# Two-layer graph attention on Trainium2: a divided tile's two sums are joined on TensorE instead of VectorE in the first half of layer 0

## The chip, the cores and the metric

The kernel runs on one core of one Trainium2 chip (trn2). A core has four engines that compute, each with its own queue of instructions, and SyncE (SP), which issues DMAs. The four are TensorE (PE, matrix products, which it adds up in PSUM), VectorE (DVE), ScalarE (ACT) and GpSimd (POOL), and POOL's queue also issues the gathers of this kernel. In the profile PEld is the loading of the stationary operand of a matmul. Each engine takes its queue in order, and waits on semaphores for the others. A layer's data pass from DRAM to the on-chip SBUF and PSUM; PSUM is where matmuls write.

The metric is device time in microseconds (us) of the whole program. The kernel before takes 2428.36 us, the median of three runs (2426.71 to 2430.07).

## The reference, cut to what matters

`x` is 8 batches of 2048 nodes with 256 features, in fp32. `adj` is a 2048 x 2048 matrix of 0 and 1 with few ones (about 17 in a row, the diagonal among them). Two layers of attention over the neighbours follow one another, each with a residual and a layer norm:

```python
    def _L0_gnn_ref(inp, adj, W1, W2, W3):
        h1 = jnp.einsum('bnc,cd->bnd', inp, W1)
        h2 = jnp.einsum('bnc,cd->bnd', inp, W2)
        h3 = jnp.einsum('bnc,cd->bnd', inp, W3)
        e = jnp.einsum('bnd,bmd->bnm', h1, h2)
        e = jax.nn.leaky_relu(e, ALPHA)
        e = jnp.where(adj[None, :, :] > 0, e, NEG_INF)
        attention = jax.nn.softmax(e, axis=-1)
        h_prime = jnp.einsum('bnm,bmd->bnd', attention, h3)
        return jax.nn.relu(h_prime)
    ...
    x = _layernorm(x + _L0_gnn_ref(x, adj, L0_gnn_W1, L0_gnn_W2, L0_gnn_W3), axis=-1)
    x = _layernorm(x + _L1_gnn_ref(x, adj, L1_gnn_W, L1_gnn_a), axis=-1)
```

The change is in layer 0. It has one attention head (layer 1 has four), and its weights multiply whole feature rows of the neighbours. Since the sum over neighbours and the product with `W3` can change places, the kernel adds up weighted rows of `x` and multiplies the sum with `W3` afterwards.

## The kernel before

**Tiles and units.** `fast_path` sorts the nodes by their number of neighbours and takes them in 16 tiles of 128 nodes, t = 0 (most neighbours, 36) to t = 15 (fewest, 11); `SLOTS` holds the largest number of each tile. The 8 batches are two halves of 4. A unit is one layer, one half and one tile: 16 units of layer 0's first half (h = 0) with t from 15 down to 0, 16 of its second half, then 32 of layer 1. In the first half VectorE also makes the list of neighbours of each tile out of a row of `adj` (`neighbours`, L613 to L631); the second half and layer 1 use the same lists.

**A slot** is the k-th neighbour of all 128 nodes of a tile. POOL gathers its 128 rows (4 batches x 256 features, 512 KB) into one of 19 ring buffers that hold two slots each (`gather`, L203). VectorE makes four dot products of it with the node's own vector `g` (`dots`, L721). When a part of a unit has all its slots, VectorE and ScalarE make the softmax weights of them. ScalarE then builds, for each slot and batch, a diagonal matrix of weights (`weighted`, L931). TensorE multiplies the gathered rows with the diagonals and adds them up in PSUM (`add_slot`, L895: eight matmuls of 64 x 64 by 256 columns a slot, four at a time in the four quarters of the array). When a chunk's last slot has been added, its ring buffer is free for the next gather.

**Divided units.** In layer 0 a unit with 16 slots or more is divided into two parts, t = 10 down to 0 in each half. The second part's softmax has a new maximum and sum, so the first part's result is a share of the whole. `sums0` runs over both parts; each has its own pair of accumulators (`u.accs[0]` and `u.accs[1]`, two PSUM tiles of 128 x 512). At the fifth slot of the second part, ScalarE scales the first part's accumulators by these shares into the buffer `u.hs` in SBUF (L1018). After the last slot, `whole` in `after0` has VectorE add the second part's accumulators to `u.hs` (L1032, two instructions). An undivided unit (t = 15 to 11) has its one pair copied out by ScalarE (L1036).

**After the sum.** `turn_h` transposes `u.hs` on TensorE (L1046), ScalarE copies the transposes out (`hT`), `project_h` multiplies with `W3` (the matmuls of L509 that write `ps_p_h`), and `residual` on VectorE applies the relu, adds the node's own row and takes the statistics (L1056, L1059). Then come the norm on ScalarE (L487), another transpose, the queries of layer 1 (`queries`, L1095) and their scatter to DRAM. Before a unit's slots `before0` does the like for `g`: `project` (the matmuls of L509 that write `ps_p_g`) and a ScalarE copy (L712).

**The order.** All engines' instructions are written out in an order made by hand. `tick` is called once for each slot of the current unit's sum; in each tick come the next slots' dot products (of later units), the next diagonals, and whatever is due. `due(n, f)` puts `f` into the order n ticks later. `after0` is called when a unit's last slot has been added, and for a divided unit sets

```python
        at = 4 if split else 2
        due(at, whole)
        due(at + 2, turn_h)
        due(at + 6, project_h)
```

so these come among the next unit's slots. `residual` is due 3 and 4 ticks after `project_h`. The instructions of one engine run in this order; between engines only data and buffers make them wait.

**The general path.** If the fast path finds that its tables don't hold the graph, it sets `flag`, and `general_path` computes everything densely. `Weights` prepares the weights for both: `products()` makes `W1 W2^T`, `terms()` makes the columns of `W` and `a` for layer 1's attention terms.

Of the kernel before, what the change touches and what calls it, by code (L numbers as in the profile page):

```python
# [139 lines left out]
def fast_path(  # L140
# [24 lines left out]
    nc = tc.nc  # L165
    B, N, C = x.shape
# [6 lines left out]
    HW = HC // 2  # L173
# [58 lines left out]
    w = Weights(nc, const, wp, ps_tile, w1, w2, w3, wq, a, C, "", (kept[:, 0], kept[:, 1]))  # L232
    ident = w.ident
# [11 lines left out]
    for it in range(NT):  # L245
        r = ring_tile(f"adj_{it}")
# [122 lines left out]
    for b in range(4):  # L369
# [6 lines left out]
        for it in range(4 * b, 4 * b + 4):  # L376
            nc.tensor.matmul(
                pm,
                lhsT=which[:, it, :],
                rhs=homes[:, it, :2].rearrange("p f s -> p (f s)"),  # L380
                start=(it == 0),
                stop=False,
# [3 lines left out]
                lhsT=which[:, it, :],  # L386
                rhs=homes[:, it, 2],
                start=False,
                stop=(it == NT - 1),
# [21 lines left out]
    for r in range(2):  # L411
        rr = slice(64 * r, 64 * r + 64)
        pr = ps_tile(f"ps_half_{r}")[:, :NT]
        for c in range(2):
            nc.tensor.matmul(
                pr[64 * c : 64 * c + 64],
                lhsT=ident[rr, rr],
                rhs=ranked[rr, 0, :],
                start=True,
                stop=True,  # L420
                tile_position=(64 * r, 64 * c),
# [70 lines left out]
    def due(distance, stage, *args):  # L492
        heappush(events, (clock[0] + distance, len(stamps), partial(stage, *args)))
        stamps.append(None)
# [406 lines left out]
                        tile_position=(64 * r, 64 * c),  # L901
                    )

    def add_extra(acc, rows, lhsT, width):
        for r in range(2):
            for j in range(2 * C // width):
                for c in range(2):
                    rhs = rows[:, ts(2 * c + j, C)]
                    if width > C:
                        rhs = rows[:, ts(c, 2 * CD)].rearrange("p (j w) -> p j w", j=2)[:, :, :C]  # L910
                    nc.tensor.matmul(
                        acc[r][64 * c : 64 * c + 64, ts(j, width)],
                        lhsT=lhsT(r, c, j),
                        rhs=rhs,
                        start=False,
                        stop=(j == 2 * C // width - 1),
                        tile_position=(0, 64 * c),
                    )

# [74 lines left out]
    def sums0(u):  # L994
        u.accs = []
        for i, part in enumerate(u.parts):
            acc = None
            for k in range(part.K):
                while len(u.diags) <= part.at + k:
                    yield 0  # L1000
                if acc is None:
                    acc = [acc_tile(f"acc_{u.name}_{i}_{r}") for r in range(2)]
                diag = u.diags[part.at + k]
                c, s = part.where(k) if k < part.main else (0, 0)
                rows, n, _ = u.chunks[i][c]
                if k < part.main:
                    add_slot(acc, k, part.K, rows[:, s, :], diag)
                else:
                    add_extra(
                        acc, rows[:, 0, :], lambda r, c, j: diag[r][:, 2 * c + j, :], C  # L1010
                    )
                if s == n - 1:
                    credits[0] += 1
                if i == 1 and k == 4:
                    u.hs = hs_rows
                    for r in range(2):
                        for j in range(2):
                            nc.scalar.activation(  # L1018
                                u.hs[:, ts(2 * r + j, C)], u.accs[0][r][:, ts(j, C)], AF.Copy,
                                scale=u.fs[:, r, j : j + 1],  # L1020
                            )
                yield 1
            u.accs.append(acc)

    def after0(u):
        h, t, n = u.h, u.t, u.name

        def whole():
            if len(u.parts) == 2:
                for r in range(2):  # L1030
                    v = u.hs[:, ts(r, HW)]
                    nc.vector.tensor_tensor(v, v, u.accs[1][r], ALU.add)  # L1032
            else:
                u.hs = hs_rows
                for r in range(2):
                    nc.scalar.copy(u.hs[:, ts(r, HW)], u.accs[0][r])  # L1036

        def turn_h():
            u.hT = wide_tile(f"hT_{n}")
            by_node = u.hT[:, :HC].rearrange("p (c j k r n) -> p j (k r) c n", c=2, j=2, k=KC, r=2)  # L1040
            for j in range(2):
                pt = ps_tile(f"ps_t_h_{n}_{j}")
                for k in range(KC):
                    for r in range(2):
                        o = r * HW + j * C + k * P
                        nc.tensor.transpose(pt[:, ts(2 * k + r, P)], u.hs[:, o : o + P], ident)  # L1046
                due(2, nc.scalar.copy, by_node[:, j], pt.rearrange("p (a c n) -> p a c n", a=4, c=2))

        def project_h():
            u.y = wide_tile(f"y0_{n}")[:, :HC]  # L1050
            u.yb = u.y.rearrange("p (b c) -> p b c", b=HB)
            u.st = sp.tile([P, 2, nc.vector.BN_STATS_DIM], F32, tag="st", name=f"st_{n}")
            project(u.hT, w.w3, f"h_{n}", 3, residual)

        def residual(i, pp):
            nc.vector.scalar_tensor_tensor(  # L1056
                u.y[:, ts(i, 512)], pp, 0.0, u.xr[:, ts(i, 512)], ALU.max, ALU.add
            )
            nc.vector.bn_stats(  # L1059
                u.st[:, i, :], u.yb[:, 2 * i : 2 * i + 2, :].rearrange("p b c -> p c b")  # L1060
            )
            if i == 1:
                mv = u.st.rearrange("p i (b s) -> p (i b) s", s=3)
                u.mv = mv[:, :, 1], mv[:, :, 2]
                rested[u.index] = clock[0]
                due(2, roots)

        def roots():
            u.z = root(u.mv, n)
            due(2, scales)  # L1070

        def scales():
            u.scales = factors(u.mv, u.z, n)
            due(2, norms, 0)
            due(3, norms, 2)

        def norms(b0):
            for b in (b0, b0 + 1):
                normalise(u.yb, u.yb, b, *u.scales)
            if b0:  # L1080
                nc.sync.dma_start(x1s[h][ts(t, P), :], u.y)
                due(2, turn_x)

        def turn_x():
            u.x1T = wide_tile(f"x1T_{n}")
            turn(u.y, f"x1_{n}", u.x1T)
            due(4, queries, 0)
            due(6, queries, 1)

        def queries(r):  # L1090
            u.qrow = q_rows
            for b in range(2 * r, 2 * r + 2):
                pq = ps_tile(f"ps_q_{n}_{b}")
                for k in range(KC):
                    nc.tensor.matmul(  # L1095
                        pq[:, : CD + H],
                        lhsT=u.x1T[:, ts(b * KC + k, P)],
                        rhs=w.sqs[:, k, : CD + H] if b == 0 else w.sqs[:, k, H:],
                        start=(k == 0),
                        stop=(k == KC - 1),  # L1100
                    )
                if b in (0, HB - 1):
                    o = 0 if b == 0 else H + b * CD
                    due(2, nc.scalar.copy, u.qrow[:, o : o + CD + H], pq[:, : CD + H])
                    continue
                o = 2 * H + HB * CD + (b - 1) * H
                due(2, nc.scalar.copy, u.qrow[:, H + b * CD :][:, :CD], pq[:, :CD])
                due(2, nc.scalar.copy, u.qrow[:, o : o + H], pq[:, CD : CD + H])
            if r == 1:
                due(3, own_terms)  # L1110

        def own_terms():
            own, o = own_d[h][ts(t, P), :], H + HB * CD
            nc.sync.dma_start(own[:, :H], u.qrow[:, :H])
            nc.sync.dma_start(own[:, H : HG - H], u.qrow[:, o + H :])
            nc.sync.dma_start(own[:, HG - H :], u.qrow[:, o : o + H])
            late.append((clock[0] + 1, store))

        def store():
            scatter(f"q{h}", qg[h][:, :], order[:, t : t + 1], u.qrow[:, H : H + HB * CD])  # L1120
            tabled[0] += 1
            if tabled[0] == 2 * NT:
                credits[0] += MORE

        split = len(u.parts) == 2
        at = 4 if split else 2
        due(at, whole)
        due(at + 2, turn_h)
        due(at + 6, project_h)
# [328 lines left out]
    for j, u in enumerate(units):  # L1458
# [9 lines left out]
        if 2 <= j < 10:  # L1468
            b, i = divmod(j - 2, 2)
# [22 lines left out]
def general_path(  # L1492
# [36 lines left out]

    w = Weights(nc, const, tp, ps_tile, w1, w2, w3, wq, a, C, "g")  # L1530
    w.products()
    w.rows_of(nc, const, 1, C)
    ident = w.ident
    mask = maskp.tile([P, NT, N], I8, tag="mask", name="gmask")
# [252 lines left out]
```

## Time and profile before

| What | Before |
|---|---|
| Timed runs, median (lowest to highest) | 2428.36 us (2426.71 to 2430.07) |
| Profiled execution, time | 2403.25 us |
| its span, first to last instruction | 2401.5 us |
| granted TensorE clock, mean | 0.899 |
| DMA moved | 717.85 MB, mean 299 GB/s |
| dot products L721 | 2248, 421 ns each |
| diagonals L931 | 2248, 344 ns each |
| matmuls of slots in layer 0, L895 with `dg` | 8992, 392 ns each |
| additions L1032 | 44, 681 ns each |

The profiled execution is one run, 25 us shorter than the median of the timed ones. The mean duration of a matmul is its time in a pipeline: in dense stretches several run at once. Layer 0's first half ends about 800 us into the span, its second half about 1375 us, and layer 1 takes the rest.

How to read the views used below. The totals give each engine's busy time, its share of the span and its number of instructions. A window gives the same between two points of time. A group names line, engine, operation and `out<-in` by the program's tile names, with the number of instructions, then busy time, mean duration in ns, and the idle time of that engine just before them with what ended it. `held` is the name under which the trace has `u.hs`, `u.g` and the query rows, which share three set-aside ring buffers; `s` is a gathered slot, `dg` a diagonal, `ident` the identity matrix. A wait names the waiting instruction, `<-`, and the one that released it.

### The profile page before, as it was taken

The numbers are of one execution on the slowest core, as the hardware profiler recorded it, in microseconds if no ns is written. First come the engines' busy times: TensorE is split into PE (matmuls) and PEld (weight loads), VectorE is DVE, ScalarE is ACT, GpSimd is POOL, SyncE is SP. The second block draws the span as 40 slices with busy tenths as digits, with TensorE's granted clock in tenths as the row PEclk, the third lists the DMA queues.
The fourth block names the chain that finished last, engine by engine and source line by source line (L and its number), as shares of the span: only waits on it lengthen the run. The fifth ranks groups of instructions, "written<-read, shape, count | busy, mean of one in ns | idle before, by whom it ended". The sixth has DMA issues, their size and how long they took to land. (4 is left out here: it accounts for less than half of the span.)

```text
span 2401.5 us, 50494 instructions
## 1 busy us (share of the span) xinstructions
PE 2006.4 (84%) x16234; PEld 1068.8 (45%) x16234; DVE 1950.7 (81%) x6799; ACT 1411.2 (59%) x4867; POOL 1407.8 (59%) x1379
## 2 busy tenths in 40 slices
PE   5158999899889999999999888888888788777885
PEld 2135566565555666666666532332233232222232
DVE  7498699988888886988989578787977788788887
ACT  6045676666667778777777655443465556343545
POOL 3354465645545556555555566666666666766663
PEclk9578999999999999999999989788888888978887
DMA  9977898878868889888888899889999899999981
GB/s 378 380 246 263 277 331 305 311 277 287 297 228 279 290 291 315 278 280 302 292 312 282 289 344 318 310 296 337 320 316 334 300 342 308 313 315 326 327 308 53
DMA packets 229919, 717.85 MB, mean 299 GB/s; under 512 B 47824, under 2 KB 57168, under 8 KB 227216
## 3 DMA queue, kind: packets, MB, share of 16 engines
q0 software_dynamic: 182272, 645.78, 76.6%
q1 hardware_dynamic: 46144, 67.65, 8.4%
q8 instruction: 132, 2.16, 0.4%
q10 hardware_dynamic: 1232, 1.11, 0.1%
q14 instruction: 139, 1.14, 0.1%
HBM read 674.46 MB, written 76.02 MB: 313 GB/s over the span
## 5 line engine op out<-in xcount | busy, mean ns | idle before, releaser
L895 PE MATMUL acc<-s,ident 64*64 64x512 f32 x4496 | 804.7, 687 | 179.7 <-issue 135.0
L203 POOL DMA_INDIRECT s<-xg,idx x564 | 591.9, 1049 | 518.1 <-PE acc L895 262.6
L721 DVE CUSTOM_DVE_ANT_0 j<-s,held 128x256 bf16<-128x256 f32 x2248 | 798.9, 421 | 54.6 <-DMA s<-xg,idx 42.9
L895 PE MATMUL acc<-s,dg 64*64 64x256 f32 x8992 | 682.3, 392 | 92.7 <-issue 42.3
L203 POOL DMA_INDIRECT s<-qg,idx x564 | 574.1, 1018 | 299.1 <-issue 150.8
L931 ACT ACTIVATE dg<-twice,e 128x64 f32<-128x64 f32 x2248 | 575.1, 344 | 64.7 <-remote 23.0
L895 PEld LDWEIGHTS acc<-s,ident 64*64 64x64 f32 x4496 | 284.3, 151 | 688.2 <-issue 608.5
L978 DVE TENSOR_TENSOR s<-s,p 128x2048 f32<-128x2048 f32 (+1 forms) x246 | 542.9, 2210 | 0.1
L895 PEld LDWEIGHTS acc<-s,dg 64*64 64x64 f32 x8992 | 377.8, 134 | 352.6 <-issue 159.0
L968 ACT ACTIVATE s<-s,e 128x64 f32<-128x64 f32 x1376 | 344.8, 342 | 81.1 <-DVE e L1234 23.4
L721 DVE DVE_READ_ACCUMULATOR2_ANT e<- 128x1 f32 x2248 | 184.1, 82 | 0.1
L211 POOL DMA_INDIRECT out_dram<-o,oidx x128 | 130.1, 1017 | 70.6 <-issue 31.6
L1436 ACT ACTIVATE e<-e 128x40 f32<-128x40 f32 (+19 forms) x88 | 27.7, 315 | 212.6 <-DVE m L1213 73.1
L1095 PE MATMUL ps_q<-wqs,x1T 128*128 128x264 f32 x512 | 138.8, 412 | 9.8 <-ACT held L1436 6.0
L509 PE MATMUL ps_p_g<-held,xT 128*128 128x256 f32 x512 | 125.7, 395 | 17.8 <-ACT xT L1436 16.3
L509 PE MATMUL ps_p_h<-held,hT 128*128 128x256 f32 x512 | 122.2, 392 | 0.1
L1436 ACT COPY held<-ps_q 128x4 f32<-128x4 f32 (+1 forms) x192 | 51.1, 311 | 115.4 <-PE ps_q L1095 96.5
L1095 PEld LDWEIGHTS ps_q<-wqs,x1T 128*128 128x128 f32 x512 | 95.4, 196 | 50.2 <-issue 22.7
L509 PEld LDWEIGHTS ps_p_g<-held,xT 128*128 128x128 f32 x512 | 97.3, 196 | 45.5 <-ACT xT L1436 16.8
L1158 DVE TENSOR_TENSOR e<-s,own 128x32 f32<-128x32 f32 (+1 forms) x290 | 52.9, 187 | 70.8 <-DMA s<-qg,idx 58.5
L509 PEld LDWEIGHTS ps_p_h<-held,hT 128*128 128x128 f32 x512 | 96.6, 194 | 26.2 <-issue 12.9
L1336 DVE TENSOR_TENSOR xr<-xr,ex 128x1024 f32<-128x1024 f32 x32 | 39.3, 1227 | 75.9 <-issue 53.0
(210 smaller groups left out, 1513.9 us busy)
## 6 DMA issues: line engine op xcount, KB each, us to landing
adj<-in_adj_dram SPq DMA_DIRECT2D x16, 1024.0 KB
x1s<-y SPq DMA_DIRECT2D x32, 512.0 KB
xr<-x1s SPq DMA_DIRECT2D x128, 128.0 KB
s<-xg,idx POOLq DMA_INDIRECT x564
s<-qg,idx POOLq DMA_INDIRECT x564
edges<-adj SPq DMA_DIRECT2D x16, 512.0 KB
xg<-in_x_dram SPq DMA_DIRECT2D x4, 2048.0 KB
xg<-in_x_dram POOLq DMA_DIRECT2D x8, 1024.0 KB
```

The lines of the kernel that those rows point to most:

```text
L203: nc.gpsimd.indirect_dma_start(out=dst, out_offset=None, in_=table, in_offset=AT(ap=index, axis=0), bounds_check=table.shape[0] - 1, oob_i ...
L211: ins = nc.gpsimd.indirect_dma_start(out=table, out_offset=AT(ap=index, axis=0), in_=src, in_offset=None)
L509: nc.tensor.matmul(pp[:, ts(j, C)], lhsT=srcT[:, ts((2 * i + j) * KC + k, P)], rhs=weight[:, k, :], start=(k == 0), stop=(k == KC - 1),)
L721: nc.vector.tensor_tensor_reduce(out=jt, in0=rows[:, ts(b, C)], in1=others(b), scale=1.0, scalar=0.0, op0=ALU.mult, op1=ALU.add, accum_out ...
L895: nc.tensor.matmul(out, lhsT=lhsT, rhs=rhs, start=(k == 0 and j == 0), stop=(k == K - 1 and (j == 1 or diag is None)), tile_position=(64 * ...
L931: nc.scalar.activation(diag[:, b, :], twice, AF.Copy, scale=u.p[i][:, b, k : k + 1])
L968: nc.scalar.activation(v[:, a, g, :], v[:, a, g, :], AF.Copy, scale=pv[:, a, g : g + 1])
L978: nc.vector.tensor_tensor(v, v, pv.unsqueeze(3).to_broadcast([P, n, H, D]), ALU.mult)
L1095: nc.tensor.matmul(pq[:, : CD + H], lhsT=u.x1T[:, ts(b * KC + k, P)], rhs=w.sqs[:, k, : CD + H] if b == 0 else w.sqs[:, k, H:], start=(k = ...
L1158: nc.vector.tensor_tensor(e[:, k : k + ns, :].rearrange("p s (b g) -> p s b g", b=HB), rows[:, :ns, :].rearrange("p s (b w) -> p s b w", b ...
L1336: nc.vector.tensor_tensor(u.xf, u.xf, u.ex, ALU.subtract)
L1436: heappop(events)[2]()
```

## The change

For a divided unit of the first half (`joined`), the last slot of the second part no longer closes the accumulation: `add_slot` and `add_extra` leave the stop flag off. A new step `join`, due at once after the unit's last slot, has TensorE multiply `u.hs` with the identity into the second part's accumulators: four matmuls with 128 rows, 64 stationary columns and 512 moving columns, two for each of the two accumulators, in the left and the right half of the array. `whole`, due four ticks after as before, then copies the two accumulators to `u.hs` on ScalarE in place of the two additions on VectorE. Units of the second half, undivided units and layer 1 keep their code. In the built program 44 matmuls (in 22 pairs) and 22 copies are added, 22 additions are gone, and everything else of the fast path stands in its old order. `general_path` now calls `w.terms()`, which adds instructions behind the branch to it.

```diff
@@ -901,7 +901,10 @@
                         tile_position=(64 * r, 64 * c),
                     )
 
-    def add_extra(acc, rows, lhsT, width):
+    def joined(u):
+        return u.h == 0 and len(u.parts) == 2
+
+    def add_extra(acc, rows, lhsT, width, last=True):
         for r in range(2):
             for j in range(2 * C // width):
                 for c in range(2):
@@ -913,7 +916,7 @@
                         lhsT=lhsT(r, c, j),
                         rhs=rhs,
                         start=False,
-                        stop=(j == 2 * C // width - 1),
+                        stop=(last and j == 2 * C // width - 1),
                         tile_position=(0, 64 * c),
                     )
 
@@ -1003,11 +1006,12 @@
                 diag = u.diags[part.at + k]
                 c, s = part.where(k) if k < part.main else (0, 0)
                 rows, n, _ = u.chunks[i][c]
+                last = not (i == 1 and joined(u))
                 if k < part.main:
-                    add_slot(acc, k, part.K, rows[:, s, :], diag)
+                    add_slot(acc, k, part.K + (not last), rows[:, s, :], diag)
                 else:
                     add_extra(
-                        acc, rows[:, 0, :], lambda r, c, j: diag[r][:, 2 * c + j, :], C
+                        acc, rows[:, 0, :], lambda r, c, j: diag[r][:, 2 * c + j, :], C, last
                     )
                 if s == n - 1:
                     credits[0] += 1
@@ -1025,8 +1029,23 @@
     def after0(u):
         h, t, n = u.h, u.t, u.name
 
+        def join():
+            for r in range(2):
+                for c in range(2):
+                    nc.tensor.matmul(
+                        u.accs[1][r][64 * c : 64 * c + 64, :],
+                        lhsT=ident[:, ts(c, 64)],
+                        rhs=u.hs[:, ts(r, HW)],
+                        start=False,
+                        stop=True,
+                        tile_position=(0, 64 * c),
+                    )
+
         def whole():
-            if len(u.parts) == 2:
+            if joined(u):
+                for r in range(2):
+                    nc.scalar.copy(u.hs[:, ts(r, HW)], u.accs[1][r])
+            elif len(u.parts) == 2:
                 for r in range(2):
                     v = u.hs[:, ts(r, HW)]
                     nc.vector.tensor_tensor(v, v, u.accs[1][r], ALU.add)
@@ -1124,6 +1143,8 @@
 
         split = len(u.parts) == 2
         at = 4 if split else 2
+        if joined(u):
+            due(0, join)
         due(at, whole)
         due(at + 2, turn_h)
         due(at + 6, project_h)
@@ -1529,6 +1550,7 @@
 
     w = Weights(nc, const, tp, ps_tile, w1, w2, w3, wq, a, C, "g")
     w.products()
+    w.terms()
     w.rows_of(nc, const, 1, C)
     ident = w.ident
     mask = maskp.tile([P, NT, N], I8, tag="mask", name="gmask")
```

## The prediction

> **What bounds the kernel now.** I read the page's totals first, then the windows, the waits of VectorE, single rows. The page alone names no bound: TensorE and VectorE are both over 80% busy.
>
> ```profile
> span 2401.5 us, 50494 instructions
> PE 2006.4 (84%) x16234; PEld 1068.8 (45%) x16234; DVE 1950.7 (81%) x6799; ACT 1411.2 (59%) x4867; POOL 1407.8 (59%) x1379
> ```
>
> The edit touches eleven tiles of layer 0's first half (t = 10 down to 0), so the question is what paces that stretch. The kernel holds its own test: the second half of layer 0 runs the same tiles on other batches, without the neighbour search on VectorE. VectorE's addition at L1032 marks the end of a tile. The timeline has it for t=10 and t=3 in the first half, then for the same two tiles in the second (start, duration, instruction, number merged):
>
> ```profile
> 351.77 1.28 DVE L1032 TENSOR_TENSOR held<-held,acc 128x512 f32<-128x512 f32 x2
> 352.97 0.42 DVE L721 CUSTOM_DVE_ANT_0 j<-s,held 128x256 bf16<-128x256 f32 x1
> ...
> 640.46 1.28 DVE L1032 TENSOR_TENSOR held<-held,acc 128x512 f32<-128x512 f32 x2
> ...
> 974.22 1.28 DVE L1032 TENSOR_TENSOR held<-held,acc 128x512 f32<-128x512 f32 x2
> ...
> 1237.62 1.28 DVE L1032 TENSOR_TENSOR held<-held,acc 128x512 f32<-128x512 f32 x2 [0.21 <-PE acc L895]
> ```
>
> The windows between these marks (length, busy time of each engine with its instructions, granted clock, DMA share, GB/s):
>
> ```profile
> core 0: us, PE busy (x) PEld busy (x) DVE busy (x) ACT busy (x) POOL busy (x), PEclk, DMA share, GB/s
> 351.77:640.46 288.69, 263.19 (x2589) 169.22 (x2589) 259.23 (x1369) 193.34 (x701) 157.54 (x151) 0.96 0.84 293
> 974.22:1237.62 263.40, 248.57 (x2590) 165.40 (x2590) 227.06 (x1198) 191.91 (x699) 147.94 (x140) 0.99 0.85 291
> ```
>
> The reader should see a near-controlled experiment: the same seven tiles, as many matmuls (2589 and 2590), as many ScalarE instructions (701 and 699), the same DMA share; VectorE has 259.23 - 227.06 = 32.2 us more to do, and the stretch is 288.69 - 263.40 = 25.3 us longer. So of each microsecond put on VectorE here about 25.3 / 32.2 = 0.79 reached the time. That is my estimate of VectorE's share of the path in the first half. It may flatter VectorE: the clock was 0.96 against 0.99, and 3% of TensorE's 263 us are 8 us; were they all on the path, 17.3 / 32.2 = 0.54 would be left. In the second half VectorE is busy 86%, in the first 90%.
>
> Against it stand VectorE's own waits in the first window (total, times, longest), nearly all at one place, the residual that follows `project_h`:
>
> ```profile
> DVE y L1056 <- PE ps_p_h L509: 19.3, 7, 5.3
> DVE rstd L477 <- ACT z L470: 5.2, 4, 2.3
> DVE j L721 <- DMA s<-xg,idx: 0.4, 1, 0.4
> ```
>
> So TensorE's line arrives last once per tile in seven of the eleven (t=10 to 4), but not in t=3 to 0; one of each:
>
> ```profile
> 577.56 0.69 DVE L1056 SCALAR_TENSOR_TENSOR y<-ps_p_h,xr 128x512 f32<-128x512 f32 x1 [5.25 <-PE ps_p_h L509]
> 717.80 0.68 DVE L1056 SCALAR_TENSOR_TENSOR y<-ps_p_h,held 128x512 f32<-128x512 f32 x1
> ```
>
> **The change part by part.** The rows, each shape apart (busy, mean ns, idle before), and the one place where matmuls of the new shape run:
>
> ```profile
> L1032 DVE TENSOR_TENSOR held<-held,acc 128x512 f32<-128x512 f32 x44 | 28.3, 681 | 1.7 <-PE ps_q L1095 1.5 <-PE acc L895 0.2
> L1036 ACT COPY held<-acc 128x512 f32<-128x512 f32 x20 | 10.6, 583 | 0.0
> L911 PE MATMUL acc<-s,a_bc 128*64 128x512 f32 x16 | 3.9, 605 | 0.6 <-DVE s L988 0.6
> ...
> 1635.02 1.94 PE L911 MATMUL acc<-s,a_bc 128*64 128x512 f32 x8
> 1636.89 1.67 PE L895 MATMUL acc<-s,ident 64*64 64x512 f32 x9
> ```
>
> *Removed from VectorE:* 22 of the 44 additions, two per tile. Two take 1.28 us, but the dot product behind them starts 352.97 - 351.77 = 1.20 us after the first, since ends overlap. 11 x 1.20 = 13.2 us off VectorE's line; at 0.79 that is 10.4 us of time, at 0.54 7.1 us, and at most 13.2.
>
> *Added to ScalarE:* 22 copies 128x512 out of PSUM, the operation and shape of L1036 (0.583 us; two in 1.05 us as merged in the timeline). 11 x 1.05 = 11.6 us of work. ScalarE has 288.69 - 193.34 = 95 us idle in the window, 13.6 per tile, most of it waiting for TensorE. In the built order the pair stands among the builders of the next tile's diagonals (L931), before, between or behind the two copies of `project_g` (L712); behind it queue those diagonals, which TensorE's slots wait for. If that cover is gone it costs 1.05 per tile.
>
> *Added to TensorE:* four matmuls per tile, 128x64 by 512 columns, fp32. Eight of this shape ran from 1635.02 until the next slot started at 1636.89: 1.87 us, so four are 0.94. They change the array's tile shape: before the like group at 1370.54 the weight loads stood still for 0.39 us. 0.94 + 0.39 = 1.33 us per tile, 14.6 us in all; the lower bound is 0.94 where the change of shape falls on one that was there anyway (`project_g` follows directly in t=10 to 7). The built order puts them one slot of the next tile behind the tile's last; behind them stand that tile's further slots, `project_g`, and through the ring buffers that slots release, POOL's gathers. Their operand was scaled four or more slots earlier, so they wait for TensorE's own order alone.
>
> TensorE and ScalarE are one line when VectorE is not: they wait for each other. That line has what VectorE leaves, 0.21. An addition there costs 0.21 x 11 x (1.33 + 1.05) = 5.5 us if both lie on it, and nothing if both fall into idle time; as only one of the two engines can be last at a time I take one addition of about 1.2, the mean of both: 0.21 x 11 x 1.2 = 2.8 us.
>
> On this price a rule of the Trainium skill speaks against the change. By "FP8 and Floating Point Precision", section TensorE Precision Notes, true fp32 takes four passes, and by "TensorE: Matmul & The Clock Gate", section Back-to-back issue gap, a 512-column matmul takes 518 cycles, 216 ns at full clock; an estimate from both is 0.86 us for each column pair and 1.73 per tile in place of 0.94, which would make the sum 1.8 us worse. The row decides.
>
> *Moved:* the transposes `turn_h` now wait for ScalarE instead of VectorE; the instruction counts of SP and POOL and their order are the same, no DMA is moved. The second accumulator is let go by ScalarE's pair in place of VectorE's, due at the same tick. *At nothing:* the changed stop flags are fields of matmuls that were there; `terms()` in the general path stands behind a branch that this input does not take (the trace has no instruction of a line between 1500 and 1700), and costs nothing unless it is taken.
>
> Sum: -10.4 + 2.8 = -7.6 us. The profiled execution took 2403.25 us, 2401.5 of it span and 1.75 around it; it would become 2395.7. The timed runs (2426.71 to 2430.07) are 25 us longer than the profiled one; I carry the difference over to their median: 2428.4 - 7.6 = **2420.8 us**. The second half and layer 1 keep their instructions and only begin earlier. The case's own range: with 0.54 and 0.46 x 11 x 1.2 = 6.1 us the gain is 1.0; with ScalarE and TensorE hidden it is 10.4: 2418 to 2427.5.
>
> A second rule weighs the two busy rows. By busy time TensorE (263 of 288.69) stands above VectorE (259) and would be the bound. The Trainium skill, "Perfetto Trace Analysis", section Identifying the Most-Contended Engine, holds matmul busy time to be a poor measure and asks for the share of weight loads, here 169 of 288.69, 59%. By the rule the new matmuls cost nothing (-10.4); by the row the rival below follows. The pair of windows agrees with the rule.
>
> **The rivals.**
> *TensorE's line gets longer (slower).* Place: the stretch from a tile's last slot to `project_h`. For it: the seven waits at L1056, 19.3 us; there VectorE's saving only lengthens the wait, and the four matmuls are in front of what it waits for. Against it: the windows' 0.79, and 30 waits of weight loads for diagonals, 13.5 us, in which a later TensorE is free. Price: seven tiles at 1.33 = +9.3, four tiles that keep 0.79 x 1.20 = -3.8; +5.5, 2434 us; with ScalarE's pair on the line in the seven, +7.4 more, 2441. It decides once VectorE's share falls below 1.33 / (1.33 + 1.20) = 0.53, or with the copies on the line below 2.38 / 3.58 = 0.66.
> *The saving is lost in waits, the additions are hidden (no change).* Seven tiles give nothing, four give 3.8, and a tile or two pay 1.33: -2 to -1, 2427. For it: the residual's wait behind each of the seven L1032 is longer than 1.20. Against it: with those waits in it (19.3 us) the first half still grew by 25.3 us under VectorE's extra work.
> *The change does not do what it says* has nothing for it: the built order shows 44 matmuls and 22 copies more, 22 additions fewer, all else in its old order.
>
> **How the numbers follow.** 0.2% of the time, 4.9 us, is about what a measurement of this kernel tells from no change. The forecast gets 0.55: its range reaches over that bound, 0.46 faster and 0.09 same. TensorE's line 0.27: 0.25 slower, 0.02 same. No change 0.18: 0.03 faster, 0.12 same, 0.03 slower. Together 0.49 faster, 0.23 same, 0.28 slower. The time is that of the forecast, 2420.8. The range goes from the whole 13.2 us saved and a little more for the spread of the runs (1.7), 2413, to TensorE's line with some of ScalarE's copies, 2437; the forecast's own 2418 to 2427.5 stands inside.
>
> **What would show it.** The 22 additions gone and the residual's total wait at L1056 in the first half: near 19 + 3 us if I am right, over 19 + 7 x 1.2 = 28 if the saving is lost there, more still if TensorE's line grew. The distance from the end of t=10 to that of t=3: 288.7 becomes some 284 (seven elevenths of 7.6 less); above 290 the rival holds. The new matmuls should take about 1.3 us per tile, the copies 1.05 with little idle before them. The same stretch of the second half must stay at 263 to 264; if that moves as much as the first, the reason is not the edit's work. I am wrong if VectorE's share of the path in the first half, for which I have one pair of windows, comes from the clock or from POOL's 11 more instructions.

## The result and the profile after

The changed kernel took 2435.65 us (median of 8 runs, 2431.53 to 2440.21) against 2427.49 of the kernel before (8 runs, the three given above among them): a ratio of 1.0045, interval 1.0032 to 1.0058, or +11 us (7.8 to 14.1). The two medians alone lie 8.2 us apart; here and below the ratio on record is used. The kernel is slower; 7.6 us less were forecast. A second set of runs gave 1.0046 (1.0030 to 1.0063).

The page after, span and busy time of each engine:

```profile
span 2430.8 us, 50660 instructions
PE 2024.4 (83%) x16322; PEld 1071.0 (44%) x16322; DVE 1938.1 (80%) x6777; ACT 1418.1 (58%) x4889; POOL 1411.8 (58%) x1379
```

The counts are those of the edit: 22 VectorE instructions fewer, 22 ScalarE instructions more. But TensorE has 88 records more, not 44. The groups of the touched lines, each shape apart:

```profile
L1035 PE MATMUL acc<-held,ident 128*64 128x512 f32 x88 | 23.8, 605 | 0.0
L1051 DVE TENSOR_TENSOR held<-held,acc 128x512 f32<-128x512 f32 x22 | 14.2, 680 | 2.1 <-PE ps_q L1114 1.7 <-PE acc L895 0.5
L1047 ACT COPY held<-acc 128x512 f32<-128x512 f32 x22 | 11.6, 577 | 0.0
L1035 PEld LDWEIGHTS acc<-held,ident 128*64 128x64 f32 x88 | 6.1, 135 | 12.2 <-issue 12.2
```

One fp32 matmul of the program leaves two records in the trace: four matmuls a tile are eight records. The first join, in TensorE's timeline:

```profile
348.68 1.08 PE L895 MATMUL acc<-s,dg 64*64 64x256 f32 x12
349.69 1.94 PE L1035 MATMUL acc<-held,ident 128*64 128x512 f32 x8
351.56 2.21 PE L509 MATMUL ps_p_g<-held,xT 128*128 128x256 f32 x9
```

The join holds the array for 351.56 - 349.69 = 1.87 us. The prediction took the like group at L911, "eight of this shape", for eight matmuls of the program and halved its 1.87 us; it was four. The table ahead of the prediction already holds this: 2248 dot products at four a slot are 562 slots, these are 4496 matmuls at eight a slot, and the table has 8992 records. ScalarE's copies (11.6 us) and the additions that went are as costed.

The windows from the end of t=10 to the end of t=3 (ScalarE's copy in the first half, VectorE's addition in the second; columns as before):

```profile
357.45:656.49 299.04, 269.55 (x2620) 169.60 (x2615) 250.87 (x1353) 198.82 (x717) 157.61 (x151) 0.95 0.81 281
991.62:1256.37 264.75, 246.99 (x2586) 165.52 (x2587) 227.24 (x1198) 189.79 (x696) 147.80 (x140) 0.98 0.85 290
```

The first half's stretch is 299 us where it was 288.69, the second half's hardly moved (263.40). VectorE's busy time fell by 259.23 - 250.87 = 8.4 us, as it should (7 x 1.20), and the stretch did not become shorter. VectorE's waits in the first window (total, times, longest):

```profile
DVE y L1075 <- PE ps_p_h L509: 22.3, 6, 5.6
DVE s L833 <- ACT e L1457: 10.2, 2, 5.7
DVE rstd L477 <- ACT z L470: 5.1, 4, 2.3
DVE y L1075 <- issue: 4.4, 1, 4.4
```

The residual now waits 22.3 us for TensorE, 19.3 before, and 4.4 us more in one tile of the seven, where the profile shows no releaser: 26.7 in all. The other new wait is at L833, the sum over the softmax weights: 10.2 us for ScalarE's `e`, where the window before has none. Altogether VectorE's idle time in the stretch grew from 29.4 to 48.2 us, by more than the 8.4 us that it was spared. One caution: the profiled execution of before lies 25 us under its own timed median, and layer 1, which the change leaves alone, takes some 11 us less in it than in the profile after (999 and 1010 us from layer 0's last residual to the end). In that it is like the two profiles of a later set whose kernel before takes 2402 us (1000 us), and unlike the three of the set at 2422 us (1010 to 1013). So the 10 us between the two stretches are not all the change's; the timed sets decide.

### The profile page after: what moved, and what is told of

Its sections match the earlier page's. It is cut to its first block, busy times and chain, and to the rows that moved or that the text cites. A ratio compares the mean times of both kernels' runs of the same rounds, so it can differ in the third digit from the quotient of the medians.

```text
span 2430.8 us, 50660 instructions
## 1 busy us (share of the span) xinstructions
PE 2024.4 (83%) x16322; PEld 1071.0 (44%) x16322; DVE 1938.1 (80%) x6777; ACT 1418.1 (58%) x4889; POOL 1411.8 (58%) x1379
## 5 line engine op out<-in xcount | busy, mean ns | idle before, releaser
L895 PE MATMUL acc<-s,ident 64*64 64x512 f32 x4496 | 809.5, 685 | 189.0 <-issue 138.4
L895 PE MATMUL acc<-s,dg 64*64 64x256 f32 x8992 | 675.9, 395 | 90.8 <-issue 43.1
L934 ACT ACTIVATE dg<-twice,e 128x64 f32<-128x64 f32 x2248 | 574.2, 342 | 65.5 <-remote 29.4
L895 PEld LDWEIGHTS acc<-s,ident 64*64 64x64 f32 x4496 | 277.3, 151 | 708.7 <-issue 617.4
L895 PEld LDWEIGHTS acc<-s,dg 64*64 64x64 f32 x8992 | 381.8, 136 | 344.7 <-issue 151.2
L1351 ACT ACTIVATE ex<-acc 128x512 f32<-128x512 f32 x60 | 33.3, 591 | 128.6 <-remote 77.7
```

The costliest lines, as they stand in the source:

```text
L895: nc.tensor.matmul(out, lhsT=lhsT, rhs=rhs, start=(k == 0 and j == 0), stop=(k == K - 1 and (j == 1 or diag is None)), tile_position=(64 * ...
L934: nc.scalar.activation(diag[:, b, :], twice, AF.Copy, scale=u.p[i][:, b, k : k + 1])
L1351: nc.scalar.activation(u.ex[:, ts(r, HW)], u.r[r], AF.Exp)
```

## The experiments

Each set of runs times its kernels beside the kernel before. One thing has to be known to read them: the kernel before holds its level within a set, but not between sets. It took 2427 and 2422 us in two sets and 2402 in one (the high level), 2180 to 2182 in four (the low level), and the same chips appear at both. So differences are taken within a set, except where the text says otherwise; "+x us" is the ratio less one, times the median of before, with its 95% interval. Where two kernels of a set are compared, their ratios are subtracted and the intervals added in quadrature. All figures from profiles rest on one execution each.

**Low level: the parts of the change**

In the first run only `w.terms()` is added to the general path of the kernel before.

> The kernel before with one line more, the call in the general path that prepares its terms; nothing else. Theory 'TensorE's line' (the joining matmuls cost 2.26 us a tile and lengthen the line of work that ends last): no difference, within 2 us of the kernel before. Rival 'not the first half at all' (the general path's instructions move the code or the start of something): +8 to +11 us, as the changed kernel has.

Measured 0.9997 (0.9988 to 1.0005): -0.7 us (-2.6 to 1.1). At this level the line costs nothing.

The join alone:

```diff
         def whole():
-            if joined(u):
-                for r in range(2):
-                    nc.scalar.copy(u.hs[:, ts(r, HW)], u.accs[1][r])
-            elif len(u.parts) == 2:
+            if len(u.parts) == 2:
```

> The changed kernel, but VectorE adds the second sum in the divided units of the first half as it did before, and ScalarE's copies are gone; so the first part is counted twice there. The join is paid and nothing is saved. If TensorE's line sets the end and VectorE's additions were worth nothing: +9 to +13 us, as the changed kernel. If both lines bear on the end, VectorE's additions being worth the 10.4 us of the prediction: +19 to +24 us (11 tiles x 2.26 us = 24.9 at most). If the recorded shares hold and only the join's size was wrong: 0.21 x 24.9 = +5 us. If ScalarE's copies are the cost: 0 to +3 us.

Measured 1.0013 (1.0005 to 1.0022): +2.8 us (1.1 to 4.8). That is under each price named for a join that lengthens TensorE's line. Its size fits the rival that blames ScalarE's copies, which the run after the next one speaks against.

The relief alone: in the changed kernel `due(0, join)` goes, the stop flags are as before, and `whole` does nothing for these units.

> The changed kernel without the joining matmuls and without ScalarE's copies: the divided units of the first half leave out the second part's sum, and VectorE has its 22 additions less. Recorded share of VectorE (0.79): -10 us. If VectorE's additions were hidden: 0 to -3 us.

Measured 0.9961 (0.9948 to 0.9974): -8.5 us (-11.3 to -5.7). VectorE's additions were not hidden here.

The relief with ScalarE's copies: as the last, but `whole` keeps its copies.

> The changed kernel without the joining matmuls; ScalarE copies the second part's sum out, so the first part is left out in the divided units of the first half. The difference to the run that has neither is the price of ScalarE's 22 copies (11.6 us of its busy time): as recorded, a fifth of it, +2.4 us; if ScalarE's copies are what costs, +10 us; if hidden, 0.

Measured 0.9957 (0.9943 to 0.9970): -9.4 us (-12.4 to -6.5). The 22 copies cost nothing that can be seen.

These four came out at the low level, and there the parts add up to a gain. So the changed kernel itself was run, and with it the join in the slots' shape with a zero block:

```diff
-                        lhsT=ident[:, ts(c, 64)],
-                        rhs=u.hs[:, ts(r, HW)],
+                        lhsT=ident[64 * r : 64 * r + 64, ts(1 - r, 64)],
+                        rhs=u.hs[64 * r : 64 * r + 64, ts(r, HW)],
...
-                        tile_position=(0, 64 * c),
+                        tile_position=(64 * r, 64 * c),
```

> The changed kernel itself, once more, beside the kernel before on the same chip. The four runs so far fell on a chip where the kernel before takes 2182 us in place of 2427, and where TensorE's matmuls follow each other without the short gaps of the first profile. If the effects found there add up (join +2.9, relief -9.2, copies 0): -6 us, ratio 0.997, so the change is faster there, by about what was predicted. If the change is slower by itself (0.45%, as first measured): ratio 1.0045 wherever it runs. On a chip like the first: ratio 1.0045 again.

> As the run with the join alone (VectorE's additions kept), but the four joining matmuls of a tile have the slots' shape of 64 x 64 with half the rows, and add a zero block; so the divided units are complete. No change of tile shape, and the four can run side by side: about 0.9 us a tile in place of 2.26. If the join's price is its time in the array: 0.4 of the price of the join alone, on the chip of the earlier runs about +1 us. If it is the wait for the first part in hs, or the change of shape: the same as the join alone (+3), or 0.

The changed kernel: 0.9981 (0.9972 to 0.9990), -4.1 us (-6.1 to -2.2). It is *faster* at the low level. The join in the slots' shape: 1.0000 (0.9990 to 1.0010). Against the join alone that is 2.8 us less (0 to 5.7, ratios of two sets on two chips), which points to the join's time or shape as the price and not to the wait for `hs`, but no more than points.

What differs between the levels is seen in the kernel before. TensorE's waits in the stretch t=10 to t=3, matmuls, first at the high level (351.77 to 640.46 of the profile before):

```profile
PE acc L895 <- issue: 14.7, 37, 1.0
PE acc L895 <- ACT dg L931: 3.2, 4, 1.1
```

and at the low level, in the run with `w.terms()` alone (331.80 to 594.76), which stands for the kernel before:

```profile
PE acc L895 <- ACT dg L931: 12.0, 10, 2.5
PE ps_q L1095 <- DVE y L1056: 9.1, 4, 4.5
PE ps_t_x L501 <- DVE y L1056: 5.2, 3, 2.0
```

At the high level TensorE's waits are on "issue" (the profile shows nothing that it waits for), and its records take longer in all: 2589 of them 263.19 us, at the low level 2586 of them 234.76. At the low level it waits for ScalarE and VectorE. VectorE's answer in the low window is one line, with no wait for TensorE at all:

```profile
DVE rstd L477 <- ACT z L470: 0.6, 1, 0.6
```

The pair of windows that the prediction rested on, at the low level (the same tiles, first and second half, same run):

```profile
331.80:594.76 262.96, 234.76 (x2586) 157.97 (x2579) 257.96 (x1367) 191.54 (x703) 160.91 (x154) 0.96 0.90 325
902.43:1132.55 230.12, 225.20 (x2632) 155.85 (x2631) 225.53 (x1199) 193.59 (x712) 151.94 (x143) 1.00 0.93 334
```

VectorE is busy 257.96 of 262.96 us, 98%: here it does set the end. The pair gives (262.96 - 230.12) / (257.96 - 225.53) = 1.01, and the relief alone shortened this stretch (from residual to residual, 263.6 to 255.4) by 8.2 of the 8.4 us that VectorE was spared. The granted clock, 0.96 in both levels' first window, doesn't explain the levels. The starts of layer 1's matmul records (L895, in groups of four, one for each quarter of the array) show where TensorE differs:

```
gaps over 300 ns between starts   inside a group   between groups
kernel before, high level               763              524
before + terms, low level                 0             1121
```

**Low level, with TensorE loaded**

To bring TensorE to the end of the line, every third slot of the divided first-half units is added twice, in four kernels:

```diff
+                if u.h == 0 and len(u.parts) == 2 and k < part.main and k % 3 == 1:
+                    add_slot(acc, k, 99, rows[:, s, :], diag)
                 if k < part.main:
```

> The kernel before with more work for TensorE alone: in the divided units of layer 0's first half every third slot is added twice (71 slots of 16 matmul records more, by 0.86 us a slot as the trace has them, 61 us over 11 tiles, 5.6 us a tile); so these units count such slots twice. On this chip a tile takes 37.6 us there, with TensorE busy 34 and VectorE 37. With 5.6 us more TensorE should set the end, as on the chip of the first measurement: +20 to +40 us against the kernel before. If VectorE still sets it: under +8.

> The changed kernel with the same doubled slots. Theory 'which engine sets the end decides the sign': here the change costs, as at first: +8 to +20 us against the kernel before with the doubled slots (11 joins x 2.26 us = 24.9, less what VectorE's relief still gives). If the change's gain and price don't depend on TensorE's load: -5 us against it, as on this chip without doubled slots.

> The join alone (VectorE's additions kept, the first part counted twice) with the same doubled slots. Same theory: +18 to +25 us against the kernel before with doubled slots, nearly the whole 24.9. If the join stays hidden: +3, as without them.

> VectorE's additions left out, without join and copies (the second part's sum is left out in those units), with the same doubled slots. Same theory: 0 to -4 us against the kernel before with doubled slots. If VectorE's relief is worth the same everywhere: -9 us.

Against the kernel before: +18.5 us (15.0 to 21.8) for the doubled slots (20 to 40 expected), +26.4 with the change, +24.9 with the join alone, +9.6 with the relief alone. So with doubled slots the change costs 7.8 us (2.6 to 13.0): its sign has turned. The parts miss their expectations: the join alone 6.3 (1.1 to 11.5) in place of 18 to 25, the relief alone -8.9 (-13.6 to -4.2) in place of 0 to -4. The relief's sign has not turned: it is worth as much with TensorE loaded as without (-8.5). The windows, before with doubled slots, the change, and the relief alone, from the residual of t=11 to that of t=4:

```profile
315.90:581.90 266.00, 263.44 (x3346) 187.57 (x3348) 258.36 (x1369) 194.68 (x707) 162.19 (x154) 1.00 0.91 325
```

```profile
313.20:585.00 271.80, 271.51 (x3311) 187.80 (x3309) 251.41 (x1359) 199.35 (x718) 161.60 (x154) 1.00 0.90 319
```

```profile
315.20:575.90 260.70, 260.68 (x3303) 185.92 (x3306) 250.39 (x1356) 194.46 (x707) 161.19 (x154) 1.00 0.92 332
```

In the first TensorE (99%) and VectorE (97%) are both nearly full; in the other two TensorE is busy all the time. The relief alone shortens the stretch by 5.3 us although TensorE is full; why, no run shows. With the join in it, VectorE's relief buys nothing (join alone 270.7, join and relief 271.8). A join with TensorE full thus takes (271.8 - 260.7) / 7 = 1.6 us a tile by the windows, the copies with it. By the timed runs of this set, the change against the relief alone, it is 16.8 us (11.7 to 21.8), 1.5 a tile (1.1 to 2.0).

Three more kernels for what was left: ScalarE's first-part copies lay the halves out so that the join can have the slots' shape, without and with doubled slots, and the change with doubled slots without the 22 copies.

```diff
+                                for c in range(2):
+                                    cc = slice(64 * c, 64 * c + 64)
+                                    nc.scalar.activation(
+                                        u.hs[64 * r : 64 * r + 64, ts(2 * c + j, C)],
+                                        u.accs[0][r][cc, ts(j, C)], AF.Copy,
+                                        scale=u.fs[cc, r, j : j + 1],
+                                    )
...
+                        lhsT=ident[64 * r : 64 * r + 64, ts(r, 64)],
+                        rhs=u.hs[64 * r : 64 * r + 64, ts(c, HW)],
...
+                        tile_position=(64 * r, 64 * c),
```

> The change made otherwise: ScalarE puts the first part into hs with the array's halves in the place that the joining matmuls need (eight copies of 64 x 256 in place of four of 128 x 256), so that the join can be four 64 x 64 matmuls of 64 rows, the slots' own shape, side by side; the whole sum is computed. Price of the join in this shape by the earlier run: 0; price of four ScalarE copies more per tile (some 0.35 us each, 15 us over 11 tiles): 0 if ScalarE's copies are hidden, as its 22 were. Theory 'the join's time in TensorE is the price': -7 to -10 us against the kernel before, where the change has -5. If ScalarE's line is near the end too: -3 to +3.

> The same with every third slot of these units added twice, so that TensorE sets the end. Against the kernel before with the doubled slots (1.0085 of the kernel before): the join now takes 0.9 us a tile in place of 2.26, so 11 x 0.9 = +10 at most in place of +25: -5 to +2 us, where the change has +9.9. If it is ScalarE's copies that cost where TensorE sets the end, +8 or more.

> The changed kernel with the doubled slots, without ScalarE's 22 copies of the joined sum (so the second part is left out in these units); the join stays, VectorE's additions stay out. With doubled slots the join alone was +9.0, the relief alone -7.3, both with the copies +9.9. If the copies are what is missing in the sum (they follow the join on the way to the transposes): -6 to -8 us against the changed kernel with doubled slots, that is 1.009 of the kernel before. If, with the join paid, VectorE's relief is worth nothing because TensorE alone sets the end: 0 to -2, that is 1.011 to 1.012.

The reshaped join: 0.9983 (0.9974 to 0.9993), -3.7 us, no better than the change's 0.9981; with doubled slots 1.0108, which is 5.0 us (0.3 to 9.7) over the kernel before with doubled slots, against 7.8 for the change: the reshaping takes away a part of the join's price at most. Beside the changed kernel it is no better beyond doubt at either load. Without the copies 1.0115, 1.3 us less than with them (6.5 less to 3.9 more): the copies are not what is missing in the sum, and what is missing stays open. From the relief alone (1.0044) to this one only the join is added: 15.5 us (10.9 to 20.1), 1.4 a tile. The differences with doubled slots in this paragraph are between ratios of two sets on two chips, both at the low level; the 16.8 us above are within one set and say the same.

**High level**

With two of every three slots doubled (`k % 3 > 0`), before and after; this set happened to run at the high level.

> The kernel before with two of every three slots of the divided units of layer 0's first half added twice (those units count them twice): 134 slots more, 115 us of TensorE by 0.86 us a slot. The first third of them cost 17 us, of which TensorE first had to fill its idle time; the next 54 us of TensorE's work should cost nearly their full time: +60 to +75 us against the kernel before.

> The changed kernel with the same slots doubled, so that TensorE alone sets the end and the join is seen at its full price. By the trace of the changed kernel (eight records a tile, 1.94 us, and the entry's idle time of 0.39): 11 x 2.26 = 24.9, so +18 to +25 us against the kernel before with the same slots. By the size that was recorded (1.33 a tile): 14.6 at most, +11 to +15. If VectorE's relief still counts there: 10 less, +8 to +15.

1.0318 and 1.0353: +76.4 us (70.1 to 82.4) and +84.8; the change costs 8.4 us (-0.5 to 17.3). The expected 18 to 25 did not come; the interval is too wide to tell the other two apart.

The last set was at the high level too (before 2422.45), with the change and its two halves as above:

> The changed kernel once more. By now the kernel before has taken 2427 us (first measurement), 2182, 2180, 2181 and 2402 us, the last two on one and the same chip; within a set of runs it holds its level. If this set is at the high level (above 2390): ratio 1.003 to 1.006, as first measured. If it is at the low level (below 2200): 0.997 to 0.999.

> The join alone once more (VectorE's additions kept, the first part counted twice). At the high level, where TensorE issues with gaps and sets the end: +8 to +16 us (1.004 to 1.006). If the change's loss at the high level comes from somewhere else: +3, as at the low level. At the low level: +2 to +3.

> VectorE's additions left out once more, without join and copies (the second part's sum is left out in those units). At the high level, if TensorE sets the end there: 0 to -4 us. If VectorE's share is the recorded 0.79 there too: -10. At the low level: -9.

The change 1.0046, +11.1 us (7.3 to 15.3); the join alone 1.0021, +5.1 us (0.7 to 9.2); the relief alone 1.0019, +4.6 us (0.5 to 8.7). The join is under its expected +8 to +16, and the relief, expected at 0 to -4 or -10, gained nothing. VectorE's waits in the relief alone, over the residuals of t=10 to t=4 (345 to 650):

```profile
DVE y L1074 <- PE ps_p_h L509: 29.3, 7, 6.7
```

Seven waits, 29.3 us; in the profile before they were 19.3. But this profile is the slowest of its twelve runs (2443 us, their median is 2429), with a granted clock of 0.92 in the stretch, so not all of that need be the relief's. The other two kernels of the set are a closer pair, with profiles near their medians and a clock of 0.95 in both. First the join alone, which keeps VectorE's additions (L1048), then the change, over the same seven waits (340 to 640):

```profile
DVE y L1072 <- PE ps_p_h L509: 14.8, 7, 3.7
DVE held L1048 <- PE ps_p_g L509: 5.0, 3, 3.4
```

```profile
DVE y L1075 <- PE ps_p_h L509: 23.4, 7, 4.3
DVE s L833 <- ACT e L1457: 8.8, 2, 5.6
```

VectorE was spared 8.4 us in the stretch, and the residual waits 8.6 us more; the wait at L833 comes on top. The timed runs agree: against the join alone, with `w.terms()` in both, the change is 6.1 us longer (0.4 to 12.1). So at this level the relief gains nothing in either comparison.

## Why the prediction was wrong

*Removed from VectorE.* The 13.2 us were right, the share of 0.79 was the step that failed: it made -10.4 us, and at the level of the measurement the relief alone is +4.6 (0.5 to 8.7). That is 15 of the 19 us between forecast (-7.6) and result (+11.1). The relief went largely where the rival had put it, into the residual's wait (14.8 us in the join alone, 23.4 in the change), and some of it into the wait at L833, which nobody had named. The sign put down for the lost saving, over 28 us of waiting at the residual, is not there in the changed kernel (26.7 and 23.4 in its two profiles); only the relief alone has it, in the slowest of its runs. The share came from one pair of windows, and such a pair tells what an engine is worth only where that engine is the one that ends last: at the low level, VectorE 98% busy and waiting 0.6 us, it gave 1.01 and in that stretch the relief delivered it (over all eleven tiles the timed relief is 8.5 of the 13.2 us). In the profile before VectorE was busy 90% and waited 19.3 us for TensorE in the same window. The lines were on the table; the ratio was believed above them.

*Added to TensorE.* The working was wrong and the price near by luck. Eight records are four matmuls, so the join's own time is 1.87 us and not 0.94. That is near the 1.73 of the estimate that was set aside for the row, made from the Trainium skill's "FP8 and Floating Point Precision", section TensorE Precision Notes, and "TensorE: Matmul & The Clock Gate", section Back-to-back issue gap. The 0.39 us for the change of shape were no price: weight loads idle as long before the first join, but TensorE's matmuls have 0.0 us of idle time before the joins; and the 0.39 at 1370.54 were ended by a diagonal from ScalarE (L945), not by the shape. With TensorE full the join costs 1.4 us a tile (1.0 to 1.8, from 15.5 us over 11) or 1.5 (1.1 to 2.0), where 1.33 was forecast; whether that is less than 1.87 the runs don't decide. Its effect at the level of the measurement, +5.1 us (0.7 to 9.2) for the join alone, holds the 2.8 forecast; the rival's 9.3 lies at its upper end, just outside.

The second rule weighed, "Perfetto Trace Analysis", section Identifying the Most-Contended Engine, was read to say that the new matmuls cost nothing. They cost 2.8 us (1.1 to 4.8) at the low level and 5.1 at the high one; matmul busy time, which the section holds to be no good measure of the distance to the roofline, was the better sign here. With the doubled slots weight loads were busy for 187.80 of 271.80 us, 69%, and TensorE had no room for the join.

*Added to ScalarE.* No cost shows: -0.9 us (-5.0 to 3.2) at the low level between the relief with and without copies, +1.3 (-3.9 to 6.5) with doubled slots. The forecast's 2.8 us stood for the join or the copies, whichever was last. The copies were not measured alone at the high level.

*At nothing.* `w.terms()` is nothing at the low level. At the high level it wasn't tried by itself, and it stands in all three kernels of the last set. So it is open whether the +4.6 us of the relief alone are the relief's, the line's, or near the nothing that their interval almost reaches. That no gain of 10 us is hidden in them is shown only as far as the change against the join alone (+6.1) shows it, which has the line in both kernels but the copies in one. Join and relief add up to the change's loss there (5.1 + 4.6 = 9.7 against 11.1), which fits each of these.

*The rivals.* "TensorE's line gets longer" had the sign, the place and the test (above 290 us from t=10 to t=3: 299.04, with the caution above) and +5.5 for its price; the runs say +11. Both engines were close to the end, and the levels go with something that the edit doesn't touch, how fast TensorE issues. That this decides the sign is argued, not shown: a TensorE loaded at the low level turned the sign of the change, but left the relief its 8.9 us, which it doesn't have at the high level. What makes TensorE issue slower in some sets than in others stays open.

## What to carry over

A share of the path worked out from two stretches holds only where the engine is busy nearly all of the stretch and waits for nobody; where the view of waits shows it waiting for another engine once per tile, work taken from it may only lengthen that wait. Moving work between two engines that are both near the end is a trade whose sign can turn with their loads (here from -4.1 to +7.8 us when TensorE got more to do): take such work to TensorE only where it has time to spare, and test each half of the trade alone, beside the kernel before and in the same set of runs. Before a row is used as a price, count how many records one instruction of the program leaves.

## What the runs showed of the hardware

- An fp32 matmul of the program stands in the trace as two matmul records, each with its weight load (44 matmuls, 88 records; 562 slots of eight matmuls, 8992 records).
- The same kernel on the same chip ran at two levels, 2181 and 2402 us on one, 2180 to 2182 and 2422 us on another, with a spread within a set of 1% at most. In layer 1 no start inside a group of four matmuls came over 300 ns behind the one before at the low level (granted clock 0.913), and 763 did at the high level (0.899).
- With TensorE busy 100% of a stretch, 1.87 us of matmuls in another tile shape cost 1.4 us a tile (1.0 to 1.8) or, within one set and with ScalarE's copies, 1.5 (1.1 to 2.0); for 22 ScalarE copies of 577 ns no cost showed (+1.3 us, -3.9 to 6.5).
